# A joint attention and MLP stage: MLP halves for the last tile pair inside the loop, downs and outputs in groups of two or three matmuls, contexts laid out by tile

## The chip, the cores and the metric

The kernel runs on one core of one Trainium2 chip. The metric is the device time of one execution in microseconds (us), and the median over several executions is what is compared. One execution was profiled: its trace gives every instruction of the five engines (PE = TensorE matmuls, PEld = TensorE weight loads, DVE = VectorE, ACT = ScalarE, POOL = GpSimd) and of the DMA queues (SP issues nearly all of them).

## The reference

A decoder of two layers on x (16 x 128 tokens of 256 numbers, so 2048 rows, held as 16 tiles of 128). Each layer is attention, cross attention and an MLP, each followed by a sum with x and a layernorm. The changed stage is layer 0's cross attention together with layer 0's MLP:

```
q = _fq_sym((x @ Wq + bq) * scale);  k, v = _fq_sym of (ctx @ Wkv + bkv)      # 16 heads of 16
attn = softmax(q k^T)                       # every row attends to all 2048 context rows
attn = _fq_unsigned(attn)                   # steps of (row maximum)/255
x = layernorm(x + (attn v) @ Wp + bp)
gate, up = split(x @ w_gate_up.T);  x = layernorm(x + (silu(gate) * up) @ w_down.T)
```

## The kernel before

The phases follow one another: layer 0's attention (0 to 808 us), the keys and values of the cross attention (814 to 889 us), the **joint stage** (889 to 1712 us), then layer 1's attention, cross attention and mixture of experts. A phase takes its SBUF from a pool that is given back at its end, so the first loads of a phase wait for the last readers of the phase before.

**The loop of the joint stage.** `steps` has 128 entries: 8 pairs of tiles (`gp`), 8 pairs of heads (`i`), 2 tiles (`u`). A pair of tiles thus takes 16 steps, and a step has two halves (`part`, the two halves of the 2048 keys). Half e of step r of a pair is written (r, e) below, as `turn = (r, end)` in the code. In each half-step, in this order of the program:

- `scores` (L750): PE makes the scores of two heads for 1024 keys, in two tiles `s`. There are three `s` tiles of two PSUM banks.
- `scaled` (L757), twice: DVE scales a tile `s` into `e` and keeps the row maximum. Between the two calls DVE does whatever has been put off to this half-step (`due(at, "DVE")`).
- in the second half, the MLP's second matmul group (`ffn_half(..., 1, ...)`), where there is one;
- `context` (L800): PE's weighted sums for an earlier head pair, 0, 6, 5 and 5 matmuls in four half-steps in turn;
- `weights8` (L778): ACT's exponential to 8 bits for the step before, and a DMA that transposes it; `spread` (L790): POOL's cast of the transposed weights to bf16 for the step before that;
- `exponent` (L769), in the second half: ACT waits for DVE's maximum of the step;
- `pair_work` (L985): what the tile pairs before and after need, at fixed half-steps.

All five engines' instruction orders are written out by hand there (`manual_schedule`, L1053): an engine runs its instructions in the program's order, so PE cannot make the scores of half-step at+1 before the `pair_work` of half-step `at` is through. `later(at, engine, f)` puts a function off to a later half-step's place on that engine.

**What `pair_work` does** in a middle pair gp: the queries of the two tiles of pair gp+1 at (0,0) and (3,1) (`query`: PE L570, then DVE L577, L579, L587 and POOL L583 to L593); for pair gp-1 the reciprocal sums are transposed (`divided`, L821) at (4,1) and (5,0), the contexts are divided by DVE one half-step later (L826), multiplied with Wp (`put_out`, L832) at (5,1) and (6,0), added to x with the layernorm's statistics (`add_output`, L838, L136, L137), normalised by POOL (`norm_pair`, L142 to L149) and transposed (`transposed`, L155) at (7,1); its MLP's gate and up halves (`ffn_half`, L870) fill the steps 8 to 15; for pair gp-2 the MLP's down projection (`ffn_put_out`, L904, added at L912) is at (1,0), (2,0), (3,0) and (4,0), and its transposition at (6,1). All of these take their PSUM tile from the tag `misc`, which has **one buffer of one bank**: the next user of it waits until DVE or ACT has read the last one's result.

**The tail.** After step 127, nine more rounds of the loop without scores run the rest of the attention of pair 7 and, in `tail_work` (L1025), all 8 units of pair 6's MLP and its downs; pair 7's MLP stands after the loop, with the gate and up weights in one load of 2 MB (`ffn_load_all`, L856). The bias bp of the cross attention is loaded at the start and added to x by POOL (L548) after each of the four layernorms of the phase before.

## Time and profile before

| | us |
|---|---|
| median of 3 runs (lowest, highest) | 2769.02 (2765.05, 2771.07) |
| the profiled execution | 2766.96 |
| its span, first to last instruction | 2765.2 |
| PE / DVE / ACT / POOL busy | 2520.2 / 1910.0 / 1473.4 / 1205.5 |
| mean granted TensorE clock | 0.973 of full speed |
| first and last `scaled` of the joint stage begin | 890.3, 1638.9 |

The shares of busy time are means over phases with different limits; PE's 91% says nothing of the joint stage by itself. In rows of groups the columns are: line, engine, operation, output <- inputs, shapes, count, busy time, mean ns, then the idle time of the engine just before and what ended it.

### The profile page before, as it was taken

The numbers are of one execution on the slowest core, as the hardware profiler recorded it, in microseconds if no ns is written. First come the engines' busy times: TensorE is split into PE (matmuls) and PEld (weight loads), VectorE is DVE, ScalarE is ACT, GpSimd is POOL, SyncE is SP. The second block draws the span as 40 slices with busy tenths as digits, with TensorE's granted clock in tenths as the row PEclk, the third lists the DMA queues.
The fourth block names the chain that finished last, engine by engine and source line by source line (L and its number), as shares of the span: only waits on it lengthen the run. The fifth ranks groups of instructions, "written<-read, shape, count | busy, mean of one in ns | idle before, by whom it ended". The sixth has DMA issues, their size and how long they took to land.

```text
span 2765.2 us, 40096 instructions
## 1 busy us (share of the span) xinstructions
PE 2520.2 (91%) x14133; PEld 1510.0 (55%) x14164; DVE 1910.0 (69%) x4393; ACT 1473.4 (53%) x2778; POOL 1205.5 (44%) x1320
## 2 busy tenths in 40 slices
PE   5999999999976779988988878999988899999998
PEld 3677777777754234434443435566655546565746
DVE  5677777877747999899988972777777753323231
ACT  3455555555533888877977872555555432213120
POOL 5644545445426778878887862322232200000000
PEclk9999999999998799999999998999999999999999
DMA  7000000000010556565655552200010011111120
GB/s 225 1 1 1 1 1 1 1 1 1 1 51 25 107 113 113 119 113 103 132 117 104 112 109 77 110 1 2 2 54 11 4 57 51 50 43 57 36 65 12
DMA packets 360185, 150.86 MB, mean 55 GB/s; under 512 B 294576, under 2 KB 341136, under 8 KB 359472
## 3 DMA queue, kind: packets, MB, share of 16 engines
q1 hardware_dynamic: 358592, 144.49, 22.8%
q0 software_dynamic: 1392, 3.81, 0.6%
q8 instruction: 112, 1.84, 0.3%
q14 instruction: 89, 0.73, 0.1%
HBM read 74.71 MB, written 2.23 MB: 28 GB/s over the span
## 4 chain that ended last, share of the span: by engine, by line
PE 68%; DVE 11%; issue 7%; POOL 5%; ACT 5%; DMA 3%; SPq 0%; DVEq 0%; POOLq 0%; ACTq 0%
PE proj L339 11%; PE gate L1540 6%; PE py L1571 6%; PE up L1540 6%; DVE e L757 5%; PE po L466 4%; PE sc L1245 3%; PE tp L1265 3%; PE o L1275 3%; PE s L750 3%; PE sc L385 2%; POOL aT L790 2%; PE o L800 2%; PE pm L456 2%; PE pm L455 2%
## 5 line engine op out<-in xcount | busy, mean ns | idle before, releaser
L790 POOL CAST aT<-at 128x2048 bf16<-128x2048 uint8 x256 | 481.2, 1893 | 87.0 <-DMA at<-a 76.3
L778 ACT ACTIVATE a<-e,snl 128x2048 uint8<-128x2048 f32 x256 | 510.7, 1995 | 3.4
L757 DVE TENSOR_SCALAR_CACHE_REDUCE e<-s,qs,smx 128x1024 f32<-128x1024 f32 x256 | 336.4, 1338 | 30.1 <-PE s L750 29.8
L757 DVE TENSOR_SCALAR_CACHE_REDUCE e<-s,qs 128x1024 f32<-128x1024 f32 x256 | 319.5, 1279 | 36.1 <-PE s L750 31.6
L800 PE MATMUL o<-aT,vq 128*32 128x512 bf16 x1024 | 261.3, 390 | 1.8 <-POOL aT L790 1.8
L750 PE MATMUL s<-kT,qT 64*128 64x512 bf16 x1024 | 197.9, 398 | 41.7 <-DVE e L757 39.3
L1544 DVE TENSOR_TENSOR h<-h,up 128x512 f32<-128x512 f32 (+1 forms) x100 | 68.7, 687 | 192.7 <-PE up L1540 189.0
L1543 ACT ACTIVATE h<-gate 128x512 f32<-128x512 f32 (+1 forms) x100 | 59.7, 597 | 220.1 <-PE gate L1540 219.9
L800 PEld LDWEIGHTS <-vq 128*32 128x32 bf16 x1024 | 85.0, 97 | 162.3 <-issue 85.1
L1540 PE MATMUL gate<-xT,w_L_ffn_w1g 128*128 128x512 f32 x352 | 167.8, 595 | 0.0
L1540 PE MATMUL up<-xT,w_L_ffn_w1u 128*128 128x512 f32 x352 | 165.4, 592 | 0.0
L1254 DVE TENSOR_REDUCE amx<-sc 128x8 f32<-128x1024 f32 x96 | 116.7, 1216 | 64.7 <-PE sc L1245 64.6
L1571 PE MATMUL py<-w_L_ffn_w2T,h 128*128 128x256 f32 x704 | 154.6, 379 | 0.0
L1257 ACT ACTIVATE pr<-pr 128x1024 f32<-128x1024 f32 x96 | 101.6, 1059 | 88.4 <-DVE pr L1256 88.4
L1266 ACT COPY prT<-tp 128x512 f32<-128x512 f32 x192 | 104.3, 584 | 76.5 <-PE tp L1265 76.1
L1571 PEld LDWEIGHTS py<-w_L_ffn_w2T,h 128*128 128x128 f32 x704 | 133.7, 190 | 18.3
L870 PE MATMUL gu<-xT,wgu 128*128 128x256 f32 x440 | 126.2, 413 | 17.9 <-ACT xT L160 8.9
L750 PEld LDWEIGHTS <-qT 64*128 64x128 bf16 x1024 | 38.4, 94 | 163.7 <-issue 159.8
L409 ACT ACTIVATE pls<-sc,lm,rms_rs 128x128 f32<-128x128 f32 x256 | 113.8, 454 | 21.7 <-DVE lm L405 21.7
L339 PE MATMUL proj<-Wlk,xT 128*128 128x512 f32 x256 | 121.1, 595 | 3.5 <-DMA Wlk<-in_L_attn_Wlk 1.3
L339 PE MATMUL proj<-Wq,xT 128*128 128x512 f32 x256 | 122.1, 600 | 0.9 <-DVE raw_Wlk L348 0.9
L466 PE MATMUL po<-Wo,mT 128*128 128x256 f32 x512 | 121.2, 380 | 1.4 <-ACT mT L458 1.4
(313 smaller groups left out, 5477.6 us busy)
## 6 DMA issues: line engine op xcount, KB each, us to landing
wgu<-in_L_ffn_gu SPq DMA_DIRECT2D x112, 128.0 KB
sh<-share SPq DMA_DIRECT2D x32, 256.0 KB
at<-a SPq DMA_TRANSPOSE x256
sh<-share SPq DMA_DIRECT2D x16, 224.0 KB
sh<-share SPq DMA_DIRECT2D x16, 192.0 KB
w_L_ffn_w1g<-in_L_ffn_w1g SPq DMA_DIRECT2D x1, 2816.0 KB
w_L_ffn_w1u<-in_L_ffn_w1u SPq DMA_DIRECT2D x1, 2816.0 KB
w_L_ffn_w2T<-in_L_ffn_w2T SPq DMA_DIRECT2D x1, 2816.0 KB
```

What stands on the lines that cost most here:

```text
L339: nc.tensor.matmul(pp.rearrange("p h d -> p (h d)"), lhsT=xTt(b, k), rhs=wts[nm, hg][:, k, :], start=k == 0, stop=k == 1)
L409: nc.scalar.activation(pls[:, h, :], by_head[:, h // 2, h % 2, NC4:NK], AF.Exp, bias=nm[:, h : h + 1], scale=rq[:, h : h + 1], accum_out=s ...
L466: nc.tensor.matmul(outs[b], lhsT=st["mT"][:, h, :], rhs=wts["Wo", hg][:, h, :], start=hg == 0 and h == 0, stop=hg == 3 and h == 3,)
L750: nc.tensor.matmul(s[hh][:, c, :], lhsT=qT[t % 4][r, i, :], rhs=kT[r, i, at : at + G], start=True, stop=True)
L757: nc.vector.tensor_scalar(st["e"][hh][:, half, :], s[hh].rearrange("p a b -> p (a b)"), qs[2 * gp + u][:, 2 * i + hh : 2 * i + hh + 1], No ...
L778: nc.scalar.activation(a.bitcast(U8), st["e"][hh].rearrange("p a b -> p (a b)"), AF.Exp, bias=st["nm"][:, hh : hh + 1], accum_out=groups[g ...
L790: nc.gpsimd.tensor_copy(aT[:, :, hh, u * P : (u + 1) * P].rearrange("p (b j) q -> p b j q", j=2), st["at"][hh].bitcast(U8).rearrange("p b ...
L800: nc.tensor.matmul(o[r : r + 32].rearrange("p a b -> p (a b)"), lhsT=vq[:, n, 32 * i : 32 * i + 32], rhs=aT[:, n].rearrange("p a b -> p (a ...
L870: nc.tensor.matmul(ffn_ps[q][:, n, :], lhsT=wt[:, k, :], rhs=xT[q // 2][:, k, at], start=k == 0, stop=k == 1)
L1254: nc.vector.tensor_reduce(mx, sc, AX.X, ALU.max)
L1540: nc.tensor.matmul(pp[:rows], lhsT=wt[:, k, :], rhs=xT[g][:, k, :], start=k == 0, stop=k == 1)
L1571: nc.tensor.matmul(py, lhsT=h[:rows, i4 * P : (i4 + 1) * P], rhs=wt, start=n == 0, stop=n == len(parts) - 1)
```

## The change

- **MLP halves.** Pair 6's gate and up halves move from the tail into steps 8 to 15 of pair 7, as for the other pairs. The tail's units (`tail_unit`) go. The first three loads of a pair's gate and up weights are issued one half-step earlier.
- **Downs.** The 32 matmuls of 128x128 per tile pair, 8 at a time at four half-steps, become 16 of 128x256 at six half-steps, (1,0) to (3,1): 3, 3, 2, 3, 3, 2. Both tiles' results lie in one PSUM tile, with one add per tile (at (2,1) and (4,0)) in the place of two. `transposed` for pair gp-2 moves from (6,1) to (5,0).
- **Outputs.** 8 matmuls with Wp, 4 at (5,1) and 4 at (6,0), become 3, 3, 2 at (5,1), (6,0), (6,1), in one PSUM tile; the adds go to (6,1) and (7,0), `norm_pair` from (6,1) to (7,0).
- **Contexts by tile.** `ot` is laid out with the tile first; both tiles are divided by one DVE instruction of 128x1024 instead of two of 128x512, and their sums are transposed together at (4,1).
- **Query.** The second query moves from (3,1) to (4,0).
- **Tail.** Pair 6's downs are at (1,0), (1,1), (4,0) of the tail, pair 7's sums start two half-steps after the last step, its division is at (4,1), its outputs at (5,1) and (6,0); the last downs use 128x256 as well.
- **bp** is loaded in the joint stage's own pool and added by POOL at the beginning of the steps 0 to 15.

In the order of the instructions of the changed program PE waits for DVE before the ninth of the 16 downs (the first that writes the second tile's half) and before the seventh of the 8 outputs, and the first load of the keys' phase no longer stands behind additions of bp, of which there are none in the phase before any more; it waits for PE, among others.

```diff
@@ -204,7 +204,6 @@
         bo = load_row(pool, w["L0_attn_bo"], "bo0")
-        bp = load_row(pool, w["L0_xattn_bp"], "bp")
...
@@ -541,11 +540,7 @@
                 if n - 5 >= 0 and (n - 5) % 16 == 15:
-                    g = (n - 5) // 16
-                    layernorm(g, ps, "tp")
-
-                    for t in range(4 * g, 4 * g + 4):
-                        nc.gpsimd.tensor_tensor(xs[t], xs[t], bp, ALU.add)
+                    layernorm((n - 5) // 16, ps, "tp")
...
@@ -607,6 +602,7 @@
             wq = load_w(pool, "L0_xattn_Wq")
+            bp = load_row(pool, w["L0_xattn_bp"], "bp")
...
@@ -736,7 +732,7 @@
             ssum = stat.tile([P, 2, 16], F32, tag="ssum", name="ssum", bufs=3)
-            ot = wk.tile([P, 2, 2, 2 * P], F32, tag="ot", name="ot")
+            ot = wk.tile([P, 2, 2, 2, P], F32, tag="ot", name="ot", bufs=1)
...
@@ -811,28 +807,30 @@
         def sums_by_dim(gp, u):
-            rb = wk.tile([P, 16, 16], F32, tag="rb", name="rb", bufs=1)
+            rb = wk.tile([P, 16, 16], F32, tag="rb", name="rb")
...
-        def sums_T(rb):
-            pt = ps.tile([P, 2, P], F32, tag="misc", name="pt_r")
-            for c in range(2):
-                nc.tensor.transpose(pt[:, c, :], rb[:, 8 * c : 8 * c + 8, :].rearrange("p h d -> p (h d)"), ident)
+        def sums_T(rbs):
+            pt = ps.tile([P, 2, 2, P], F32, tag="misc", name="pt_r")
+            for u, rb in enumerate(rbs):
+                for c in range(2):
+                    nc.tensor.transpose(
+                        pt[:, u, c, :], rb[:, 8 * c : 8 * c + 8, :].rearrange("p h d -> p (h d)"), ident
+                    )
...
-        def divide(gp, u, pt):
-            own = groups[gp][2][:, :, :, u * P : (u + 1) * P]
-            nc.vector.tensor_tensor(own, own, bc(pt, 2, 2), ALU.mult)
-
-        def output(gp, u):
+        def divide(gp, pt):
+            ot = groups[gp][2].rearrange("p u c h q -> p (u c) h q")
+            nc.vector.tensor_tensor(ot, ot, bc(pt.rearrange("p u c q -> p (u c) q"), 2, 2), ALU.mult)
+
+        def output(gp, js, py):
             ot = groups[gp][2]
-            py = ps.tile([P, HID], F32, tag="misc", name="py")
-            for c in range(4):
+            for j in js:
+                u, c = j // 4, j % 4
                 nc.tensor.matmul(
-                    py, lhsT=ot[:, c // 2, c % 2, u * P : (u + 1) * P], rhs=wp4[:, c, :], start=c == 0, stop=c == 3
-                )
-            return py
+                    py[:, u, :], lhsT=ot[:, u, c // 2, c % 2, :], rhs=wp4[:, c, :], start=c == 0, stop=c == 3
+                )
...
@@ -895,23 +893,19 @@
-        def ffn_down(q, u, c, tag="misc"):
-
-            at = slice(c * P, (c + 1) * P)
-            pp = ps.tile([P, 2, G] if tag == "s" else [P, P], F32, tag=tag, name="pd", bufs=3 if tag == "s" else 1)
-            pd = pp[:, 0, 0:P] if tag == "s" else pp
-            for i in range(NI):
+        def ffn_down_psum(tag="misc"):
+            pp = ps.tile([P, 2, G] if tag == "s" else [P, G], F32, tag=tag, name="pd", bufs=3 if tag == "s" else 1)
+            return (pp[:, 0] if tag == "s" else pp).rearrange("p (u d) -> p u d", u=2)
+
+        def ffn_down(q, js, pd):
+            for j in js:
+                u, i = j // NI, j % NI
                 nc.tensor.matmul(
-                    pd, lhsT=hs[q][:, i, u * P : (u + 1) * P], rhs=wd[:, i, at], start=i == 0, stop=i == NI - 1
-                )
-            return pd
-
-        def ffn_add(q, u, c, pd):
-            t = 2 * q + u
-            x = xs[t][:, c * P : (c + 1) * P]
-            nc.vector.tensor_tensor(x, x, pd, ALU.add)
-            if c == 1:
-                norm_pair_stats(t)
+                    pd[:, u], lhsT=hs[q][:, i, u * P : (u + 1) * P], rhs=wd[:, i, :], start=i == 0, stop=i == NI - 1
+                )
+
+        def ffn_add(q, u, pd):
+            add_output(2 * q + u, pd[:, u])
...
@@ -948,29 +942,45 @@
-        def divided(gp, u, at):
-
-            pt = sums_T(rbs.pop((gp, u)))
-            later(at + 1, "DVE", divide, gp, u, pt)
-
-        def put_out(gp, u, at):
-            py = output(gp, u)
-            later(at + 1, "DVE", add_output, 2 * gp + u, py)
-            if u == 1:
+        def divided(gp, at):
+
+            pt = sums_T([rbs.pop((gp, u)) for u in range(2)])
+            later(at + 1, "DVE", divide, gp, pt)
+
+        pys = {}
+
+        def put_out(gp, js, at):
+
+            if 0 in js:
+                pys[gp] = ps.tile([P, 2, HID], F32, tag="misc", name="py")
+            output(gp, js, pys[gp])
+            for u in range(2):
+                if 4 * u + 3 in js:
+                    later(at + 1, "DVE", add_output, 2 * gp + u, pys[gp][:, u])
+            if 7 in js:
...
             ffn_gate(q, i, n)
+            if 2 * i + n + 3 < 2 * NI:
+                ffn_load(2 * i + n + 3)
...
-        def ffn_put_out(q, u, c, at, tag="misc"):
-            pd = ffn_down(q, u, c, tag)
-            later(at + 1, "DVE", ffn_add, q, u, c, pd)
-            if (u, c) == (1, 1):
+        pds = {}
+
+        def ffn_put_out(q, js, at, tag="misc"):
+
+            if 0 in js:
+                pds[q] = ffn_down_psum(tag)
+            ffn_down(q, js, pds[q])
+            for u in range(2):
+                if NI * u + NI - 1 in js:
+                    later(at + 1, "DVE", ffn_add, q, u, pds[q])
+            if 2 * NI - 1 in js:
...
@@ -987,61 +997,42 @@
             turn = (r, end)
-            if gp < LAST and turn in ((0, 0), (3, 1)):
-                query(2 * gp + 2 + r // 3, at)
+            if gp < LAST and turn in ((0, 0), (4, 0)):
+                query(2 * gp + 2 + r // 4, at)
             if gp > 0:
-                if turn in ((4, 1), (5, 0)):
-                    divided(gp - 1, r - 4, at)
-                elif turn in ((5, 1), (6, 0)):
-                    put_out(gp - 1, r - 5, at)
+                if turn == (4, 1):
+                    divided(gp - 1, at)
+                elif turn in ((5, 1), (6, 0), (6, 1)):
+                    j = 3 * (2 * r + end - 11)
+                    put_out(gp - 1, range(j, min(j + 3, 8)), at)
...
                     transposed(gp - 1, at)
-            if 0 < gp < LAST:
-                j = 2 * (r - 8) + end
-                if -3 <= j < 0:
-                    ffn_load(j + 3)
+                if turn in ((6, 0), (6, 1), (7, 0)):
+                    ffn_load(2 * r + end - 12)
...
                     ffn_half(gp - 1, r - 8, 0, at)
-                    if j + 3 < 2 * NI:
-                        ffn_load(j + 3)
-
-            if 1 < gp <= LAST:
-                if not end and 1 <= r <= 4:
-                    ffn_put_out(gp - 2, (r - 1) // 2, (r - 1) % 2, at)
-                elif turn == (6, 1):
+
+            if gp > 1:
+                if (1, 0) <= turn <= (3, 1):
+                    j = (0, 3, 6, 8, 11, 14, 16)[2 * r + end - 2 :]
+                    ffn_put_out(gp - 2, range(j[0], j[1]), at)
+                elif turn == (5, 0):
...
-
-        def tail_unit(q, i, at, stream):
-            for m in range(2):
-                ffn_gate(q, i, m, "s")
-                if stream and 2 * i + m + 3 < 2 * NI:
-                    ffn_load(2 * i + m + 3)
-            th, gu = ffn_tiles(q, i, tail=True)
-            ffn_out(q, th, gu)
-            ffn_sigmoid(th)
-            later(at + 1, "DVE", ffn_mult, q, i, th, gu, nc.vector)
...
             turn = (r, end)
-            q = LAST - 1
-            if turn in ((1, 0), (1, 1), (2, 0)):
-                for i in range(2):
-                    tail_unit(q, 2 * (2 * r + end - 2) + i, at, True)
-            elif turn == (3, 1):
-                tail_unit(q, 6, at, True)
-            elif turn in ((4, 0), (4, 1)):
-                divided(LAST, end, at)
-                if end:
-                    tail_unit(q, 7, at, True)
-            elif turn in ((5, 0), (5, 1)):
-                put_out(LAST, end, at)
-            elif r == 6:
-                for c in range(2):
-                    ffn_put_out(q, int(end), c, at, "s")
+            if turn in ((1, 0), (1, 1), (4, 0)):
+                j = {(1, 0): (0, 4), (1, 1): (4, 8), (4, 0): (8, 16)}[turn]
+                ffn_put_out(LAST - 1, range(*j), at, "s")
+            elif turn == (4, 1):
+                divided(LAST, at)
+            elif turn in ((5, 1), (6, 0)):
+                j = 4 * (r - 5)
+                put_out(LAST, range(j, j + 4), at)
...
@@ -1056,6 +1047,8 @@
                         group(n // 16)
+                    if n < NB:
+                        nc.gpsimd.tensor_tensor(xs[n], xs[n], bp, ALU.add)
...
@@ -1071,10 +1064,8 @@
                     gp, r = n // 16, n % 16
-                    if part == 1 and 0 < gp < LAST and r >= 8:
+                    if part == 1 and 0 < gp <= LAST and r >= 8:
                         ffn_half(gp - 1, r - 8, 1, at)
-                        if 2 * (r - 8) + 4 < 2 * NI:
-                            ffn_load(2 * (r - 8) + 4)
...
@@ -1088,11 +1079,17 @@
                                 if i % 4 == 3:
-                                    later(at + 1, "ACT first", nc.scalar.copy, groups[gp][2][:, i // 4], os.pop((gp, i // 4)))
-                                if i == 7:
+                                    later(
+                                        at + 1,
+                                        "ACT first",
+                                        nc.scalar.copy,
+                                        groups[gp][2][:, :, i // 4].rearrange("p u h q -> p h u q"),
+                                        os.pop((gp, i // 4)).rearrange("p h (u q) -> p h u q", u=2),
+                                    )
+                                if i == 7 and gp < LAST:
...
                                     for u in range(2):
-                                        later(at + 1 + u, "POOL", by_dim, gp, u)
+                                        later(at + 1, "POOL", by_dim, gp, u)
...
@@ -1108,14 +1105,14 @@
                     due(at, "SP")
+                    if (n, part) == (len(steps), 1):
+                        later(at + 1, "DVE", sums, LAST)
+                        for u in range(2):
+                            later(at + 2, "POOL", by_dim, LAST, u)
...
                         tail_work(n, bool(part))
-                    if n == len(steps) - 2 + part:
-                        ffn_load(part)
-                if n == len(steps) - 1:
-                    ffn_load(2)
...
@@ -1130,9 +1127,9 @@
             for u in range(2):
-                for c in range(2):
-                    ffn_add(LAST, u, c, ffn_down(LAST, u, c, "s"))
-            norm_pair(LAST)
+                ffn_put_out(LAST, range(NI * u, NI * u + NI), 0, "s")
+                due(1, "DVE")
+            due(1, "POOL")
```

## The prediction

> **What bounds the kernel now.** I read the page's groups first, then busy time by stretches of the joint stage, then DVE's timeline and waits in one tile pair, then the chain of waits at both ends of the stage. The groups give the two costliest DVE rows:
>
> ```profile
> L757 DVE TENSOR_SCALAR_CACHE_REDUCE e<-s,qs,smx 128x1024 f32<-128x1024 f32 x256 | 336.4, 1338 | 30.1 <-PE s L750 29.8
> L757 DVE TENSOR_SCALAR_CACHE_REDUCE e<-s,qs 128x1024 f32<-128x1024 f32 x256 | 319.5, 1279 | 36.1 <-PE s L750 31.6 <-ACT snl L769 2.2 <-ACT gu_s L889 1.6
> ```
>
> DVE is the loop's pacemaker, and 61.4 us of its idle time end with scores from PE. Where, by stretches: steps 0-7 and 8-15 of pair 4, steps 8-15 of pair 7, and the tail (from, to and length, then busy PE, PEld, DVE, ACT and POOL, the granted clock, DMA):
>
> ```profile
> 1262.01:1314.21 52.20, 43.34 (x228) 20.92 (x228) 46.89 (x88) 36.26 (x44) 41.40 (x42) 0.97 0.48 92
> 1314.21:1358.19 43.98, 41.55 (x192) 18.02 (x192) 40.65 (x66) 43.03 (x65) 38.44 (x30) 1.00 0.74 144
> ...
> 1600.60:1640.30 39.70, 29.89 (x125) 8.26 (x125) 39.64 (x66) 35.78 (x43) 30.52 (x17) 0.96 0.58 112
> 1640.30:1711.80 71.50, 60.01 (x312) 46.58 (x310) 22.61 (x55) 25.51 (x56) 13.31 (x20) 0.93 0.24 68
> ```
>
> With nothing beside it DVE needs 39.7 for eight steps (third line). The first eight of a pair lose time on both accounts: more DVE work and DVE idle. DVE's timeline shows the two largest holes of pair 4 (start, length, idle before), and its waits in 1262 to 1314.2 the sum of all five:
>
> ```profile
> 1300.20 1.28 DVE L757 TENSOR_SCALAR_CACHE_REDUCE e<-s,qs 128x1024 f32<-128x1024 f32 x1 [1.52 <-PE s L750]
> ...
> 1305.75 1.34 DVE L757 TENSOR_SCALAR_CACHE_REDUCE e<-s,qs,smx 128x1024 f32<-128x1024 f32 x1 [2.03 <-PE s L750]
> ```
> ```profile
> DVE e L757 <- PE s L750: 5.2, 5, 2.0
> ```
>
> The two follow the outputs at (5,1) and (6,0), a third of 1.09 at 1288.96 the downs at (4,0): in each PE stands in front of the one `misc` bank until DVE has emptied it, then makes its matmuls, and only then the next scores. The same wait in the first eight steps of pairs 2 to 6 is 7.2, 6.0, 5.2, 5.6 and 6.1 (30.1), of pair 1 2.2, of pair 7 2.9: 35.2 in all.
>
> The chain at the stage's beginning, and in its tail:
>
> ```profile
> 805.49 2.01 PE po L466 x8
> ...
> 811.86 2.09 POOL x L548 x3
> 813.97 0.38 SPq L89
> ...
> 814.40 7.43 DMA ctxT<-in_ctxT
> ```
> ```profile
> 1665.67 8.44 DMA wgu_all<-in_L_ffn_gu
> ...
> 1681.56 7.14 PE pd L904 x64
> ...
> 1689.81 14.10 PE gu L870 x64
> ```
>
> The keys' phase begins when the last addition of bp gives the pool free. The tail is a chain of loads, contexts (PE o L800, 3.56 for 16) and MLP matmuls, with the transfer of 2 MB open in it.
>
> **The change, part by part** (us; minus is a gain).
>
> *MLP halves into pair 7: +4.8.* Eight such steps take 43.98 (pair 4) or 44.94 (pair 5), without halves 39.70; the mean difference is 4.8, the bounds 4.3 and 5.3. SP's 16 loads more stand among the transposes as in pairs 1 to 6, so that price holds them. The loads' earlier start puts one issue of 0.57 (SP at 1305.21) ahead of a transpose: nothing, since the cast that uses it runs a half-step ahead of the contexts.
>
> *The loop's first eight steps: -22.6.* Of the seven users of `misc` that remain in a pair (query, downs, query, sums, transposition, outputs, transposition; twelve before), I follow PE and DVE through the half-steps. PE needs 0.45 for the scores (four matmuls, two at a time), 0.216 for a context, 0.43 for a matmul with Wp or a down of 128x256 (two records of 0.216 each); DVE 2.41 and 2.53 for a half-step, 0.84 more for a query, 1.01 for an add with statistics (1301.41 to 1302.43). (1,0): 0.45 + 5 x 0.216 + 3 x 0.43 = 2.8 of PE against 2.41 of DVE, but PE comes out of (0,1), where DVE takes 3.3 and PE 1.75, with its scores done, and (2,0) costs PE 1.3: no idle to (2,1). There the ninth down waits for the add of the first tile, which ends 1.65 after the half-step's start; with three downs and the scores PE then comes 0.5 late in (3,0). (4,0) and (4,1): add and query on DVE cover PE's wait for each. (5,0): the division ends 2.45 after the start, transposition 0.45, scores 0.45 and their latency 0.39 against DVE's 3.7: 0.2 late at most. (6,1): the last two outputs wait for the first tile's add too, but DVE's own 3.5 there covers PE's 3.1. (7,1): statistics end 2.3 after (7,0) begins, POOL's `norm_pair` takes 2.6 (1292.03 to 1294.66), the transposition then ends 2.0 after (7,1) begins: 0.4 late. That is 1.1 per pair. POOL's cast behind this `norm_pair` comes 1.9 late, and its contexts are 5 us away; price if that cover went, the same 1.9 per pair. `ot`'s single buffer is read last at (6,1) and written again at (12,0): nothing.
>
> To the 1.1 I add 0.9 for TensorE's clock. After a stretch with long holes PE runs at half speed for one stretch of 3.4:
>
> ```profile
> 1299.40:1302.84 3.44, 1.63 (x9) 0.98 (x9) 2.57 (x6) 3.44 (x3) 3.35 (x4) 1.00 0.14 27
> 1302.84:1306.26 3.42, 3.42 (x11) 1.40 (x10) 1.39 (x3) 0.29 (x2) 1.18 (x1) 0.50 0.96 194
> ```
>
> New holes of 2.1 stand at (5,0) (PE behind the division) and (7,1), so I keep about one such stretch per pair; it costs at most half of itself, 1.7, and 0.9 is the middle between that and none. New idle 2.0 in each of pairs 2 to 7 and 1.2 in pair 1, 13.2 against 35.2: -22.0. DVE's own work: adds 0.20 + 0.88 + 0.20 + 0.88 become 2 x 1.01, and the divisions 0.54 + 0.60 one of 128x1024, by the nearest row (L1256) 1.22 less the 0.1 that overlaps: -0.1 per pair, -0.6. Bounds: 0, if the new waits are as long as the old, and -35.8, if none is left.
>
> Two rules of the Trainium skill bear on this. The Trainium skill's page "TensorE: Matmul & The Clock Gate" (Why this matters for your kernels) asks for no PE-idle gap over some 3 us between bursts. The row above speaks against reading that as enough: PE's longest gap before the half-speed stretch was 1.8 (1300.07 to 1301.88). By the rule the 0.9 goes and the sum is 6 lower; by the row it stays. The Trainium skill's page "PSUM — Partial Sum Buffer" (PSUM bank collisions raise a hardware error) says that accesses of two engines must be kept apart by bank and quadrant, not by address. That speaks against two tiles' downs in one bank: it is the wait of the ninth down. No run here shows that wait; separate banks would save the 0.5 per pair, 3 in all.
>
> *bp: -6.3.* With no addition left, the first load waits for PE's last matmul at 807.5 in place of POOL at 813.97, and everything to the loop follows 7.4 of ctxT: -6.4, less the 0.1 of the semaphore. If it waits for ACT's xT (812.1), -1.9; I take the first, since PE stands among that load's waits and the layernorm's tiles lie in no pool that is given back. The 16 additions (0.722 each, 11.6) go to POOL's steps of pair 0, where POOL has two casts, 3.8 of 4.94: nothing; uncovered it would be 11.6.
>
> *The tail: -18.4.* Before: 71.6 from DVE's last score (1640.16) to 1711.80. After: the last cast ends 9.7 after that score (1649.87); contexts 3.6; eight downs of pair 6, 3.5; sums' transposition 0.45, then add and division on DVE 2.2; outputs 3.6; add and statistics 1.05; `norm_pair` 2.65; transposition and copy 1.2; gates 14.1; downs 6.9; add 0.5: 49.4. The 2 MB are issued when the previous cast tile is read (some 7 after the score) and land 8.4 later, 11 before the gates. PE stands idle for 3.4, 2 and 5 us on the way, so half speed comes back: +4, between 0 and 8 (contexts doubled 3.6, gates 3.4, outputs 1). 71.6 - 53.4 = 18.2, with 0.2 for the adds halved.
>
> *Query at (4,0):* the same instructions, its DMA one half-step later and nine steps before its reader: nothing.
>
> Sum: 4.8 - 22.6 - 6.3 - 18.4 = -42.5. From the profiled execution (2766.96) that is 2724.5; the median of the runs stands 2.1 above that execution: **2726**.
>
> **Rivals.**
> 1. *Half speed eats the loop's gain.* Two more half-speed stretches per pair at the full 1.7, 3.4 x 5 = 17: 2743. For it: PE is emptier than before at (4,0) and (7,0). Against: of the fifteen stretches of 3.4 in pair 4's first eight steps one was slow.
> 2. *PE stays at full speed*: idle 0.5 per pair, the tail without its 4: -32.3 - 22.4 - 6.4 + 4.8 = -56: 2713. For it: the downs fill (1,0) to (3,1) more evenly. Against: the half-speed row above. With gaps of 2.1 the loop would also stay warm by the Trainium skill's page "TensorE: Matmul & The Clock Gate" (Why this matters for your kernels).
> 3. *Slower: the one `misc` bank.* If each of the five hand-overs from (2,1) to (7,1) costs what the worst cost before (2.03), DVE idles 10 in each of 7 pairs, 70 against 35.2: +35 + 4.8 - 6.3 - 18.4 = +15: 2784. It decides from (35.2 + 19.9) / 7 = 7.9 per pair, 1.6 per hand-over. For it: downs and outputs now hold the bank for six and three half-steps. Against: nobody else asks for it there.
>
> **How the numbers follow.** Chances: forecast 0.62 (own range 2714 to 2738), rival 1 0.17, rival 2 0.13, rival 3 0.06, no change 0.02. 2708 to 2748 takes in the forecast and most of rivals 1 and 2 with the bounds of the tail. A difference of 0.2% (5.5 us) is about what a measurement here tells from none. Faster 0.92, within 0.02, slower 0.06.
>
> **What will show it.** DVE's wait for scores in a pair's first eight steps near 2 in place of 6; pair 7's second eight near 44.5; the first load of the keys at 807.6; from the last score to the stage's end near 53. I am wrong if the holes at (5,0) and (7,1) exceed 1, if half-speed stretches come twice a pair, or if the loop's POOL falls behind its casts.

## The result

The changed kernel takes 2731.06 us (median of 4 runs, 2727.62 to 2733.81) against 2768.49 for the kernel before in the same comparison (4 runs, 2765.05 to 2771.07): a ratio of **0.9865, with the 95% interval 0.9848 to 0.9882**, some 37 us faster. The forecast was 2726, with the range 2708 to 2748. Its profiled execution took 2732.66, with a span of 2730.9. Below, "loop" is the time from the first `scaled` row's start to the last one's end, "tail" from there to the end of the stage's last down; all times are in us.

| profiled executions | before | changed | moved | forecast |
|---|---|---|---|---|
| first `scaled` row begins | 890.3 | 882.6 | -7.7 | -6.3 |
| loop, pair 0 | 84.2 | 81.6 | -2.7 | 0 |
| loop, first eight steps of pairs 1 to 7 | 360.4 | 344.7 | -15.7 | -22.6 |
| loop, second eight steps of pairs 1 to 7 | 305.3 | 312.5 | +7.2 | +4.8 |
| tail | 71.5 | 56.3 | -15.2 | -18.4 |
| all behind it | 1053.5 | 1053.2 | -0.3 | 0 |
| sum | | | -34.3 | -42.5 |

Every term that was forecast has the sign and the order of size of the forecast; three of them are 2 to 7 worse. The parts are read from one execution of each kernel: the first `scaled` row begins at 882.6 to 885.3 in the thirteen kernels below that have the new loading of bp, so a unit or two of a part can be chance.

The two costliest DVE rows of the changed kernel, from the page's groups:

```profile
L753 DVE TENSOR_SCALAR_CACHE_REDUCE e<-s,qs,smx 128x1024 f32<-128x1024 f32 x256 | 335.0, 1334 | 16.9 <-PE s L746 15.9
...
L753 DVE TENSOR_SCALAR_CACHE_REDUCE e<-s,qs 128x1024 f32<-128x1024 f32 x256 | 319.8, 1280 | 36.7 <-PE s L746 31.2
```

DVE's wait for scores has fallen from 61.4 to 47.1. The stretches that answer to those of before are the first and the second eight steps of pair 4, the second eight of pair 7, and the tail (from, to and length, then busy PE, PEld, DVE, ACT and POOL, the granted clock, DMA):

```profile
1242.14:1292.47 50.33, 43.23 (x196) 18.76 (x196) 47.13 (x84) 36.43 (x46) 41.23 (x42) 0.97 0.55 105
1292.47:1338.36 45.89, 44.37 (x192) 19.16 (x192) 40.65 (x64) 42.94 (x65) 39.14 (x30) 0.93 0.64 127
1575.75:1621.40 45.65, 44.07 (x190) 19.17 (x191) 40.64 (x64) 42.69 (x64) 39.13 (x30) 0.93 0.62 128
1621.40:1677.70 56.30, 45.30 (x184) 32.30 (x182) 13.43 (x35) 17.02 (x35) 15.30 (x22) 0.91 0.22 52
```

In the first line DVE idles 3.2 (50.33 less 47.13) where it idled 5.3. In the second and third the granted clock is 0.93, where it was 1.00 and 0.96: the second eight steps of pairs 1 to 7 now hold nine stretches of 3.4 at half speed where they held four, and that is part of their 7.2. DVE's timeline of pair 4 shows what became of the two holes of 1.52 and 2.03; these are now the three longest of its first eight steps, and the waits of the same stretch sum them up:

```profile
1262.65 1.34 DVE L753 TENSOR_SCALAR_CACHE_REDUCE e<-s,qs,smx 128x1024 f32<-128x1024 f32 x1 [0.62 <-PE s L746]
...
1273.12 1.28 DVE L753 TENSOR_SCALAR_CACHE_REDUCE e<-s,qs 128x1024 f32<-128x1024 f32 x1 [0.57 <-PE s L746]
...
1280.21 1.28 DVE L753 TENSOR_SCALAR_CACHE_REDUCE e<-s,qs 128x1024 f32<-128x1024 f32 x1 [0.62 <-PE s L746]
```
```profile
DVE e L753 <- PE s L746: 2.3, 5, 0.6
DVE e L753 <- ACT snl L765: 0.4, 1, 0.4
```

Holes of 1.5 to 2 have become holes of 0.6, and one of 0.4 in which DVE waits for ACT's `exponent` of the step before.

On PE the change is less plain. These are PE's waits in the first eight steps of pair 5 (1338.36 to 1389.12): in us, how many, and the longest.

```profile
PE pq L565 <- DVE x L836: 1.8, 1, 1.8
PE ln_pt L155 <- POOL x L149: 1.6, 2, 1.4
PE ln_pt L155 <- DVE ot L825: 1.5, 1, 1.5
PE pd L903 <- DVE x L836: 0.8, 1, 0.8
PE py L831 <- DVE x L836: 0.8, 1, 0.8
PE pq L565 <- ACT gu_s L887: 0.5, 1, 0.5
```

They sum to 7.0; the same stretch of the kernel before has 8.6 in nine rows. So PE still stands in front of the one `misc` bank: at (4,0) for the query behind the downs' last add, at (5,0) for the division, and at (2,1) and (6,1) for the first tile's add. At (7,1) it waits not for the bank but for `norm_pair` on POOL. What was won is that DVE notices it less.

At the boundary, SP's queue and its waits show the first load of the keys, 7.0 earlier than at 813.97:

```profile
806.93 0.38 SPq L89 DMA_DIRECT2D w_L_xattn_Wkv<-in_L_xattn_Wkv  x1
```
```profile
SPq L89 <- PE po L465: 5.1, 1, 5.1
```

It waits for PE's last matmul of the phase before, as forecast.

### The profile page after: what moved, and what is told of

The parts are those of the page before. It is cut to its first block, busy times and chain, and to the rows that moved or that the text cites. A ratio compares the mean times of both kernels' runs of the same rounds, so it can differ in the third digit from the quotient of the medians.

```text
span 2730.9 us, 39531 instructions
## 1 busy us (share of the span) xinstructions
PE 2518.5 (92%) x13877; PEld 1493.5 (55%) x13908; DVE 1902.3 (70%) x4353; ACT 1473.7 (54%) x2778; POOL 1215.0 (44%) x1336
## 5 line engine op out<-in xcount | busy, mean ns | idle before, releaser
L746 PE MATMUL s<-kT,qT 64*128 64x512 bf16 x1024 | 191.0, 397 | 31.8 <-DVE e L753 28.7
L868 PE MATMUL gu<-xT,wgu 128*128 128x256 f32 x448 | 135.4, 427 | 9.2 <-ACT xT L160 4.3
L1253 DVE TENSOR_TENSOR pr<-sc,amx 128x1024 f32<-128x1024 f32 x96 | 117.0, 1219 | 5.7
```

The lines of the kernel that those rows point to most:

```text
L746: nc.tensor.matmul(s[hh][:, c, :], lhsT=qT[t % 4][r, i, :], rhs=kT[r, i, at : at + G], start=True, stop=True)
L868: nc.tensor.matmul(ffn_ps[q][:, n, :], lhsT=wt[:, k, :], rhs=xT[q // 2][:, k, at], start=k == 0, stop=k == 1)
L1253: nc.vector.tensor_tensor(pr, sc, bc(mx, 2, P), ALU.subtract)
```

## The experiments

Each kernel ran beside the kernel before on the same chip, in four comparisons in which the kernel before took 2765.5 to 2770.2; so times of different rows are best compared by their ratios. Medians, ratios to the kernel before with their 95% intervals, and loop and tail of the profiled execution:

| kernel | median | ratio | loop | tail |
|---|---|---|---|---|
| before | 2768.5 | 1 | 750.0 | 71.5 |
| changed | 2731.1 | 0.9865 [0.9848, 0.9882] | 738.8 | 56.3 |
| bp alone, on the kernel before | 2761.4 | 0.9968 [0.9957, 0.9979] | 752.5 | 71.7 |
| changed, MLP of pair 6 in the tail | 2741.3 | 0.9897 [0.9875, 0.9919] | 730.9 | 70.6 |
| changed, downs with a pause | 2733.2 | 0.9883 [0.9866, 0.9899] | 737.6 | 59.8 |
| changed, transposition moved | 2731.0 | 0.9880 [0.9866, 0.9895] | 743.1 | 56.8 |
| changed, outputs in two half-steps | 2728.1 | 0.9865 [0.9851, 0.9880] | 731.5 | 56.9 |
| changed, PE's wait at (7,1) filled | 2726.0 | 0.9857 [0.9843, 0.9872] | 730.6 | 54.5 |
| the same, half the filling (one execution) | 2726.1 | | 732.9 | 55.0 |
| three waits filled | 2718.7 | 0.9817 [0.9801, 0.9832] | 726.8 | 54.0 |
| (7,1) filled, DVE's small work first | 2719.4 | 0.9819 [0.9801, 0.9837] | 725.4 | 53.0 |
| the same with half the downs | 2715.6 | 0.9805 [0.9782, 0.9828] | 719.9 | 54.9 |
| the same (all downs), and the tail reworked | 2718.2 | 0.9818 [0.9801, 0.9834] | 725.8 | 50.9 |
| changed, DVE's small work first | 2718.5 | 0.9817 [0.9800, 0.9833] | 723.8 | 57.0 |

Two of them undo or isolate whole parts of the change; the others ask why loop and tail gained less than was forecast. The theory after the first reading was the clock: PE's waits at (4,0) and (7,1) set off half speed behind them. Its rivals were the wait of the ninth down for the shared bank, and plain work: PE has as much to do in these steps as DVE.

### bp alone

The row bp is loaded beside Wq and added in pair 0 instead of after the layernorms of the phase before, and `ot` has one buffer (the load and `ot` are not shown):

```
                         group(n // 16)
+                    if n < NB:
+                        nc.gpsimd.tensor_tensor(xs[n], xs[n], bp, ALU.add)
...
-                    for t in range(4 * g, 4 * g + 4):
-                        nc.gpsimd.tensor_tensor(xs[t], xs[t], bp, ALU.add)
```

> The kernel before with the bp part alone: the row of bp loaded with the joint stage's weights, its sixteen additions in the steps of pair 0 on POOL, and ot in one buffer so that the row finds room. In the kernel before the first scaled row stands at 890.3 and pair 0 takes 84.2; in the changed kernel 882.6 and 81.6. Theory A, the boundary's gain is the early give-back of the pool and nothing else of the change bears on it: the first scaled row at 882.6, pair 0 between 81.6 and 84.2, all behind it as in the kernel before, the time 7 to 10 below it (ratio 0.9965 to 0.9975). Theory B, POOL pays for the additions in pair 0 (11.6 in all): pair 0 at 86 or more, and the ratio 0.998 to 1.002.

The first `scaled` row begins at 883.9, 6.4 earlier; pair 0 takes 83.2; the time falls by 8.8. Theory A holds, and POOL does not pay for the additions. The 0.3% is a gain of its own.

### The MLP of pair 6 back in the tail

```
-                if r >= 8 and not end:
+                if gp < LAST and r >= 8 and not end:
                     ffn_half(gp - 1, r - 8, 0, at)
...
-            if turn in ((1, 0), (1, 1), (4, 0)):
-                j = {(1, 0): (0, 4), (1, 1): (4, 8), (4, 0): (8, 16)}[turn]
-                ffn_put_out(LAST - 1, range(*j), at, "s")
+            if turn in ((1, 0), (1, 1), (2, 0)):
+                for i in range(2):
+                    tail_unit(q, 2 * (2 * r + end - 2) + i, at, True)
+            elif turn == (3, 1):
+                tail_unit(q, 6, at, True)
...
+                if r == 6:
+                    ffn_put_out(q, range(16), at, "s")
```

> The changed kernel with the MLP of the last pair but one put back where the kernel before has it: no halves in pair 7's second eight, its units in the tail between the contexts, its loads there; downs, outputs and the rest of the loop stay as changed. In the changed kernel pair 7's second eight take 45.7 and the tail (last scaled row to the last down) 56.3; in the kernel before 39.7 and 71.5. Theory A, the halves cost 4.3 to 6 in pair 7 and save 13 to 16 in the tail: second eight at 39.7 to 40.5, tail at 69 to 72, the time 8 to 11 above the changed kernel. Theory B, half of the 6 is the half speed that the wait at (7,1) leaves behind at (8,0), and comes without halves too: second eight at 42 to 43, the time 11 to 14 above. Theory C, the tail's gain comes mostly from its own new order: tail at 60 to 64, the time at most 3 above.

The second eight steps of pair 7 and the tail of this kernel:

```profile
1575.07:1615.99 40.92, 32.40 (x125) 8.45 (x124) 39.79 (x64) 35.55 (x42) 30.72 (x17) 0.83 0.53 103
1615.99:1686.63 70.64, 60.49 (x248) 44.60 (x247) 22.36 (x51) 25.54 (x56) 13.33 (x18) 0.93 0.25 70
```

40.9 against 45.7 with the halves, and 70.6 against 56.3: the halves cost 4.7 and save 14.3, and the time is 10.2 above the changed kernel's (8.9 by the ratios). Theory A holds with its second eight steps 0.4 over the bound; C falls. B asked for 42 to 43 and gets only its cause: there is half speed here too, but with no gates to make DVE hardly feels it (39.79 busy of 40.92).

### Downs with a pause

```
-                    j = (0, 3, 6, 8, 11, 14, 16)[2 * r + end - 2 :]
+                    j = (0, 4, 8, 8, 11, 14, 16)[2 * r + end - 2 :]
```

> The changed kernel with the downs at another pace: four each at (1,0) and (1,1), none at (2,0), then three, three and two at (2,1), (3,0) and (3,1), so that the first tile's add at (2,0) has the bank for itself. The loop (first scaled row to the end of the last) takes 738.7 in the changed kernel, and its half-steps (1,0) to (3,1) take 17.7 in the mean of pairs 2 to 6; DVE's own work in them is 15.8. Theory A, the ninth down's wait for the shared bank (0.85 of PE, and what follows it) is the loss: the six half-steps take 16.3 to 16.8, about 1.1 less in each of six pairs, and the loop 732. Theory B, PE has too much to do in these half-steps, whatever the order (four downs, five contexts and the scores are 3.25 of PE against 2.47 of DVE): the holes move to (1,1) and (2,0), the six half-steps stay within 0.3 of 17.7, the loop at 737 to 740.

The half-steps (1,0) to (3,1) of pair 5, here first in the changed kernel, then with the pause:

```profile
1344.09:1361.75 17.66, 16.61 (x77) 7.88 (x76) 16.42 (x32) 13.36 (x17) 15.02 (x13) 1.00 0.59 112
```
```profile
1341.70:1359.36 17.66, 16.25 (x77) 7.99 (x76) 16.38 (x32) 13.36 (x17) 14.32 (x12) 1.00 0.54 104
```

PE's wait of 0.8 at the ninth down is gone from its list, and the six half-steps take 17.66 as before. The hole has moved, as DVE's timeline shows: it now idles before (2,0), after four downs each at (1,0) and (1,1). PE's scores begin at 1343.41 and 1347.05 with no wait between them, so such a half-step is 3.64 of PE, and not the 3.25 of the expectation:

```profile
1347.79 1.28 DVE L753 TENSOR_SCALAR_CACHE_REDUCE e<-s,qs 128x1024 f32<-128x1024 f32 x1 [1.00 <-PE s L746]
```

Theory B holds. The wait of the ninth down was there and cost nothing that this other order of the downs gives back.

### The transposition moved out of (5,0)

```
-                elif turn == (5, 0):
-                    transposed(gp - 2, at)
+                elif gp > 2 and turn == (0, 1):
+                    transposed(gp - 3, at)
```

> The changed kernel with the transposition after the downs taken from (5,0), between the division's factors and the outputs, to (0,1) of the next pair (for the last pair into the tail). In the changed kernel PE waits 1.9 at (5,0) for the division to give the bank free, and (5,0) and (5,1) take 3.77 and 3.31 in the mean of pairs 2 to 6; DVE's work in them is 3.6 and 2.5. Theory A, a user of the bank fewer between division and outputs saves its wait: 0.8 to 0.9 less in each of six pairs at (5,0) and (5,1), little at (0,1), whose query makes DVE slow anyway, and the loop takes 734. Theory B, the wait only moves: (0,1) and (1,0), now 3.32 and 2.41, become 0.5 to 1 longer since the transposition waits for the query's read and the first down for the copy behind it, and the loop takes 737 to 741.

(5,0) and (5,1) take 0.93 less in the mean of pairs 2 to 6 (3.54 and 2.61), and (1,0) and (1,1) 0.88 more (2.94 and 3.22). PE's waits in the first eight steps of pair 5 say the same; the division's 1.5 is gone, and in its place the same transposition waits for the query's read:

```profile
PE ln_pt L155 <- DVE qa L572: 0.9, 1, 0.9
```

The wait only moved: theory B. The loop is 4.3 longer than the changed kernel's in these two executions: pair 0, which the edit does not touch, takes 3.0 more, (8,0) and (8,1) together 3.2 more (half speed stands there in six of seven pairs, in four of them for two stretches), and the first eight steps 2.4 less. The median is the same, the ratio 0.9880 against 0.9865 with intervals that overlap.

### Outputs in two half-steps

```
-                elif turn in ((5, 1), (6, 0), (6, 1)):
-                    j = 3 * (2 * r + end - 11)
-                    put_out(gp - 1, range(j, min(j + 3, 8)), at)
+                elif turn in ((5, 1), (6, 0)):
+                    j = 4 * (r - 5)
+                    put_out(gp - 1, range(j, j + 4), at, 2)
```

The last argument puts the first tile's add a half-step later, beside the second one's.

> The changed kernel with the outputs in two half-steps, four at (5,1) and four at (6,0), both adds at (6,1), and norm_pair behind them at (6,1) in place of (7,0). In the changed kernel (5,1) to (8,1) take 22.3 in the mean of pairs 2 to 6, of which DVE's work is some 19.3, and the loop 738.7. Theory A, norm_pair at (7,0) is too late for the transposition at (7,1), and PE's wait there sets off the half speed at (8,0) and (8,1): both go, (8,0) and (8,1) take 5.5 in place of 6.5, (7,1) 2.6 in place of 3.0, the seven half-steps 20.5, and the loop loses 9 to 12, to some 728. Theory B, PE's work is what counts and the half speed comes from how little PE has to do in (6,1) and (7,0) rather than from the wait: (8,0) and (8,1) stay at 6.5 or rise, four outputs in a half-step make holes of 1 to 2 at (5,1) and (6,0) as in the kernel before, and the loop takes 738 to 746.

(8,0) and (8,1) take 5.1 to 5.7 in six of seven pairs and 7.3 in one; before this edit 5.4 to 8.3. (5,1) to (8,1) take 21.7 in place of 22.3, with (6,1) at 4.50 for its two adds. The loop of the profiled execution falls by 7.3: theory A in kind, smaller in size, since the half speed has in part only moved to (7,0) (three pairs). The time does not show it: the ratio is that of the changed kernel.

### PE's wait at (7,1) filled

```
     def norm_pair_T(q, psum, tag, fill=0, w=None):
         pt = psum.tile([P, 2, 2, P], F32, tag=tag, name="ln_pt")
+        for _ in range(fill):
+            nc.tensor.matmul(pt[:, 0].rearrange("p a b -> p (a b)"), lhsT=ident, rhs=w[:, 0, :], start=True, stop=True)
```

with `fill` = 4 at (7,1) and the weights `wp4`; a second kernel has `fill` = 2.

> The changed kernel with four matmuls of 128x256 (1.7 of PE) more at (7,1), ahead of the transposition, into the tile that the transposition then writes over: they have no use but to keep PE busy while it waits for POOL's norm_pair; the output is the same. Theory A, the wait at (7,1) sets off the half speed behind it: the stretches of half speed at (7,1) to (8,1) (in six of seven pairs) go, (8,0) and (8,1) take 5.5 in every pair in place of 8.3 in pairs 1, 4 and 7 and 6 in the others, and the loop loses 8 to 12, from 738.7 to about 729. Theory B, (8,0) and (8,1) are long for the gates' own reasons (they wait for the copy of xT, and for the one bank between two units), whatever the clock: no change, 738 to 740, or up to 3 more where the fillers come late.

> The changed kernel with two filling matmuls (0.86) at (7,1) in place of four (1.7) or none; PE then stands idle there for some 0.6 in place of 1.4. Theory A, it is the length of the wait that sets off the half speed, and 0.6 is short enough (waits of 0.5 to 0.8 stand at (2,1) and (6,1) in every pair without a slow stretch behind them): (8,0) and (8,1) at 5.4 in every pair as with four. Theory B, it is PE's share of work in the stretch, and half of it is too little: one or two of the seven pairs still show 6 to 8.3.

PE's timeline of pair 4 around (7,1), in the changed kernel and with four filling matmuls (L154, two records each; contexts, scores and gates stand two lines lower there, at L798, L748 and L870):

```profile
1288.03 1.25 PE L796 MATMUL o<-aT,vq 128*32 128x512 bf16 x5
1290.70 0.33 PE L155 MATMUL ln_pt<-ident,x 128*128 128x128 f32 x1 [1.43 <-POOL x L149]
...
1293.07 2.07 PE L868 MATMUL gu<-xT,wgu 128*128 128x256 f32 x4 [0.74 <-ACT xT L160]
```
```profile
1285.69 1.25 PE L798 MATMUL o<-aT,vq 128*32 128x512 bf16 x5
1286.88 1.99 PE L154 MATMUL ln_pt<-wp,ident 128*128 128x256 f32 x8
1288.71 0.76 PE L157 MATMUL ln_pt<-ident,x 128*128 128x128 f32 x4
1289.40 0.61 PE L748 MATMUL s<-kT,qT 64*128 64x512 bf16 x4
1290.74 1.13 PE L870 MATMUL gu<-xT,wgu 128*128 128x256 f32 x4 [0.73 <-ACT xT L162]
```

The same four gate matmuls take 2.07 and 1.13. (8,0) and (8,1) together, with the clock in the column behind the engines:

```profile
1292.47:1300.76 8.29, 7.69 (x23) 3.33 (x24) 5.12 (x9) 7.04 (x10) 6.13 (x4) 0.59 0.55 105
```
```profile
1290.14:1295.54 5.40, 4.80 (x23) 2.19 (x24) 5.03 (x8) 5.40 (x9) 4.24 (x3) 1.00 0.45 83
```

With the filling, both half-steps take 5.38 to 5.41 in all seven pairs, where the changed kernel has 5.4 to 8.3; the loop falls by 8.2, to 730.6. Theory A was 729. Two filling matmuls do the same (5.39 to 5.43 in every pair; the loop's 732.9 has a pair 0 that took 3.2 longer with the same code). So work without any use makes these half-steps shorter, and the cause is the clock and not the gates' own waits: the wait of 0.73 for ACT's copy is still there. In the time the gain is not clear of noise: 0.9857 against 0.9865, some 2 us, with overlapping intervals; the runs with more filling show it.

### Three waits filled

To the four at (7,1) come four filling matmuls at (4,0) ahead of the query, into the score tile that is used next, and eight ahead of the tail's transposition.

> The kernel with the four filling matmuls at (7,1), four more at (4,0) of pairs 2 to 6 ahead of the query (into the score tile that comes next) and eight ahead of the transposition in the tail (PE stands idle there for 3.4). With the fillers at (7,1) alone the loop takes 730.6, with half speed after (4,0) in three pairs, and the tail 54.5. Theory A, each wait of PE of 1.8 to 3.4 sets off the half speed behind it, and any work in it prevents that: no half speed in (4,0) to (4,1) and none in the tail's gates, loop 727 to 729 and tail 52.5 to 53.5, 3 to 5 less in all. Theory B, only the wait at (7,1) mattered, since (4,0) has slack behind it: loop 730 to 732, tail at 54 to 55.

The loop takes 726.8, with one stretch of half speed left, at (5,0) of pair 7, and none in the tail's gates; the tail, 54.0, keeps half speed in its contexts. Theory A, with the tail 0.5 over its bound. In all, fillers took 11.9 from the loop (1.7 from the first eight steps of pairs 1 to 7, 10.0 from the second eight): that is what half speed costs the changed kernel there, less what the fillers themselves take. The time agrees: from 0.9865 to 0.9817, 13 us. Even so the first eight steps of pairs 2 to 5 take 49.5, with 47.0 of DVE's work: **2.5 of idle time per pair that the clock has no part in**.

### DVE's small work first

```
-                        scaled(*now, part, 0, states[n], s)
                         due(at, "DVE")
+                        scaled(*now, part, 0, states[n], s)
                         scaled(*now, part, 1, states[n], s)
```

This was run together with the fillers at (7,1), and by itself on the changed kernel.

> The kernel with the four filling matmuls at (7,1), and in addition DVE's small work of a half-step (adds, query, division) ahead of both scaled rows instead of between them. With the fillers alone the loop takes 730.6. Theory A, PE's waits for DVE's read of the one bank (0.85 at (2,1), 1.9 at (4,0), 1.9 at (5,0), 0.9 at (6,1)) are what is left of the loss, and DVE reading 1.3 earlier takes most of them: 2 to 3 less in each of six pairs, loop 713 to 719. Theory B, PE's work in these half-steps is the bound and the scores come late either way; DVE's small work first only holds back the release of the score tiles: the loop between 728 and 736.

> The changed kernel with DVE's small work of a half-step ahead of both scaled rows, without any filling matmul. With the fillers too the loop takes 725.4, with the fillers alone 730.6, the changed kernel 738.7. Theory A, the earlier read of the bank shortens PE's wait at (4,0) and (5,0), and with norm_pair 1.3 earlier that at (7,1), so that the half speed goes by itself: loop 725 to 729 and (8,0) and (8,1) at 5.1 to 5.4. Theory B, the wait at (7,1) stays near 1 to 1.4 and with it the half speed: (8,0) and (8,1) at 6 to 8 in most pairs, loop 732 to 737.

By itself it beats the changed kernel and the one with the fillers at (7,1): 2718.46, and the loop takes 723.8. The first eight steps of pairs 1 to 7 fall from 344.7 to 332.9, DVE's idle time in them from 19.5 to 10.0. PE's waits in pair 5 (1335.57 to 1383.76) are of another kind now:

```profile
PE s L746 <- DVE e L753: 3.6, 6, 1.4
PE ln_pt L155 <- DVE ot L825: 0.7, 1, 0.7
PE pq L565 <- DVE x L836: 0.5, 1, 0.5
```

The waits of the kinds shown for the changed kernel have fallen from 7.0 to 1.2; for the rest PE waits until DVE has emptied a score tile, so it runs ahead and DVE sets the pace. From pair 1 on no stretch of the loop is at half speed any more. But the clock is the smaller part in the first eight steps: the fillers took 1.7 from them, this order 11.8, so most of that is the order itself. That is theory A; only (8,0) and (8,1) are at 5.7 where 5.1 to 5.4 was expected. Together with the fillers the kernel has no half speed either, but 725.4, between its two theories: with the small work first `norm_pair` comes earlier, the four fillers end too late for the transposition, and (7,1) takes 3.74 in place of 2.60. Three waits filled and small work first end at the same ratio, 0.9817, and the second adds no work.

### Half the downs

```
                 u, i = j // NI, j % NI
+                if i % 2 and q < LAST - 1:
+                    continue
```

> The kernel with the four filling matmuls at (7,1) and DVE's small work first, with every second down of the pairs 0 to 5 left out (eight of sixteen matmuls; their share of the MLP's sum is missing from the output). That is 3.45 less of PE in (1,0) to (3,1) of pairs 2 to 7, with the same hand-overs, the same adds and the same work on DVE. Theory A, in these half-steps PE's work at full speed is the bound, not the waits: the twelve rows from the one of (1,0) to the last of (3,1), now 18.4, shrink by 1.5 to 2.6 to about 16.2 (DVE's own work is 15.8), and the loop from 725.4 to 710 to 716. Theory B, the hand-overs of the bank are the bound: at most 0.5 less per pair, loop 722 to 725.

The rows from (1,0) to (3,1) with all downs (pair 5), and with half of them (pair 4), both at full speed:

```profile
1338.68:1357.11 18.43, 17.86 (x84) 8.68 (x82) 17.25 (x34) 14.25 (x18) 15.09 (x13) 1.00 0.55 107
```
```profile
1243.79:1261.21 17.42, 15.23 (x67) 6.01 (x66) 17.09 (x35) 14.25 (x18) 14.11 (x12) 1.00 0.55 107
```

1.0 less, and 0.8 in the mean of pairs 2 to 7: between the two theories. The expectation had DVE's own work wrong: it is 17.1 in these rows (with the small work first the query's read and the second add fall into them), not 15.8. Measured by DVE's idle time, 1.18 becomes 0.33 with the same hand-overs of the bank: most of what idle time there is comes from PE's work and not from the bank, in this order of DVE's. In pairs 2, 4, 5 and 7 half speed came back, where PE was emptier and nothing else was changed, and took part of the gain; the loop won 5.4.

### The tail reworked

Small work first and four fillers at (7,1); in the tail six fillers into the free bank ahead of the last contexts, eight ahead of the transposition, and the two tiles' outputs in two banks.

> The kernel with the four filling matmuls at (7,1) and DVE's small work first, and in addition three things in the tail: six filling matmuls into the free misc bank while PE waits for the last casts, eight ahead of the last transposition, and the outputs of the two tiles in two score tiles in place of one bank, so that the second tile's do not wait for the first one's add. Without these the loop takes 725.4 and the tail 53.0. Theory A, the tail is a chain on PE with half speed after two of its waits and one hand-over of the bank (0.5 of wait and more behind it): tail 49 to 51, the time 2 to 4 below the 2719.4 of the kernel without them, 2715 to 2717. Theory B, the fillers end too late for what they wait beside, or the clock has recovered before the gates: tail 52.5 to 54, the time at 2718 to 2721.

PE's timeline of the tail in the changed kernel, from the last contexts on, and of this one:

```profile
1632.83 5.30 PE L796 MATMUL o<-aT,vq 128*32 128x512 bf16 x16 [2.97 <-POOL aT L786]
...
1644.16 1.99 PE L831 MATMUL py<-wp,ot 128*128 128x256 f32 x8 [1.94 <-DVE ot L825]
1646.67 1.99 PE L831 MATMUL py<-wp,ot 128*128 128x256 f32 x8 [0.51 <-DVE x L836]
1652.02 1.44 PE L155 MATMUL ln_pt<-ident,x 128*128 128x128 f32 x4 [3.36 <-POOL x L149]
```
```profile
1617.36 2.75 PE L1039 MATMUL warm<-wp,ident 128*128 128x256 f32 x12
1620.28 3.61 PE L798 MATMUL o<-aT,vq 128*32 128x512 bf16 x16 [0.17 <-POOL aT L788]
...
1629.92 3.72 PE L833 MATMUL py<-wp,ot 128*128 128x256 f32 x16 [1.94 <-DVE ot L827]
```

The contexts take 3.61 in place of 5.30, the outputs have no wait between the tiles, and the tail takes 50.9 in place of 53.0 without the three edits: theory A in the trace. In the time it does not show: 2718.15 against 2719.44 with intervals of 4 to 5 on either side.

## Why the prediction was right, and where its steps were off

**The sign, the range and the bound.** DVE was the pacemaker, its holes came from PE standing in front of the one bank, and the change took most of them. The time lies 5 above the forecast.

**MLP halves into pair 7 (+4.8): right.** The experiment that takes them out again gives 4.7. The trace has 6.0, and two stretches of half speed in pair 7's (8,0) and (8,1); with the wait at (7,1) filled the same eight steps take 42.8 to 43.1, which is 3.1 to 3.5 above the kernel before. So half speed is 2.5 to 2.9 of the 6.0, less what the fillers take.

**bp (-6.3): right.** -7.7 in the trace, -6.4 in the kernel that changes nothing else, -5.0 to -7.7 in all thirteen kernels that have it. The choice between PE (807.5) and ACT (812.1) as the last reader was right: the first load stands at 806.93.

**The loop's first eight steps (-22.6): the mechanism right, the term too large by 6.9.** Measured -15.7: DVE's idle time fell by 16.5 (36.0 to 19.5) and its work rose by 0.8. Three parts of the step were off.

- "No idle to (2,1)", and 0.5 at (3,0). In (1,0) to (3,1) DVE idles 1.24 (17.66 less 16.42). The price of PE was too low: a half-step with five contexts and three downs was put at 2.8, and it takes 3.24 at full speed and without a wait (the rows of (1,1) of pair 5 stand below this list; its scores begin at 1345.38, the next ones at 1348.62). DVE needs 2.41 there, so PE falls behind by 0.8 and not by 0.4, and its lead is gone sooner. Over the six half-steps PE is busy for 16.25 to 16.61 and DVE for 16.4: two engines with equal work that wait for each other now and then cannot both be full. The pause shows that moving the one named wait gives nothing, and the run with half the downs (with DVE's small work first) shows in DVE's idle time that it is mostly PE's work.
- New idle 1.1 per pair without the clock. With the waits filled it is 2.5, what the fillers themselves hold up included; this is the largest error of the sum. In pair 4 the holes stand before (3,1), (5,0) and (6,0), 0.62, 0.57 and 0.62 long, and before (8,0), 0.25. The second one stands behind the waits at (4,0) and (4,1), which were to be covered by DVE's add and query. All are below 1, the bound that was set for (5,0) and (7,1).
- The clock, 0.9 per pair in the first eight steps. There it was too much: only three stretches of half speed stand in these steps (six in the kernel before), and filling takes 1.7 from them where the sum has 5.4 (six times 0.9). But the loop has twelve in the seven pairs, 1.7 per pair, and nine of them stand behind the wait at (7,1), in (8,0) and (8,1). There they lengthen the second eight steps, which the sum has as unchanged in pairs 1 to 6. That the two errors on the clock and on PE's price go opposite ways in the first eight steps is luck. Rival 1 named the clock, and half-speed stretches "twice a pair" was one of the signs against the forecast: 1.7 comes close to it. Yet the kernel before has ten of them in the same pairs, so the change added two and moved the others.

PE's timeline of (1,1) of pair 5 in the changed kernel, for the first of the three:

```profile
1345.38 0.64 PE L746 MATMUL s<-kT,qT 64*128 64x512 bf16 x4
1345.95 1.25 PE L796 MATMUL o<-aT,vq 128*32 128x512 bf16 x5
1347.13 1.56 PE L903 MATMUL pd<-w_L_ffn_d,h 128*128 128x256 f32 x6
1348.62 0.61 PE L746 MATMUL s<-kT,qT 64*128 64x512 bf16 x4
```

**The tail (-18.4): too large by 3.2.** Contexts begin 11.4 behind the last score and not 9.7, because POOL does the last unit's two `ffn_mult` rows (0.73 each) ahead of the last casts: work that the change itself had moved there. The outputs take 4.5 in place of 3.6, with the second tile waiting 0.51 for the first one's add in the shared bank; transposition and copy take 2.1 in place of 1.2, gates 15.8 in place of 14.1. The allowance of 4 for half speed held the gates' 1.7 and the contexts' 1.7.

**Pair 0 (nothing forecast, -2.7).** Not a gain of the change: with the same work in pair 0, the kernels run here take 81.1 to 85.0 there. It goes with how long pair 0 is at half speed: the kernels at 81.1 to 81.6 have 24 to 27 us of it at half speed, those at 84.2 to 85.0 37 to 41.

**The two rules.** What the Trainium skill's page "PSUM — Partial Sum Buffer" (PSUM bank collisions raise a hardware error) asks for shows here as a wait that the program makes, and not as a loss: the ninth down's 0.8 is in the trace, and a kernel without it is no faster. The Trainium skill's page "TensorE: Matmul & The Clock Gate" (Why this matters for your kernels) asks for no PE-idle gap over some 3 us; here the measurement decides against it as sufficient: the stretch from 1288.99 to 1292.40, whose longest gap was 1.43, was followed by 6.8 us of half speed, and filling that gap removed it in every pair. What I held against rival 1 (one slow stretch in fifteen before) counted stretches and did not ask how full they were.

**What stays open.** How the 2.5 of idle time divides between PE's work, the hand-overs of the bank and ACT's `exponent` (0.4 per pair in the waits) was only argued: half the downs point at PE's work, the small work first at the hand-overs. And why one order gives a stretch just under half full that is followed by half speed and another, equally full, one that is not.

## What to carry to other kernels

When two engines have nearly equal work and one shared bank between them, do the short read that frees the bank first and the long rows after it: one line moved took 13 us off the changed kernel (by the ratios), where another pace of the downs took nothing. Ask of every wait of TensorE not how long it is but how full it leaves the 3.4 us around it, since what comes behind a stretch that is only half full can run at half speed; that loss shows up in the next stage, not where the wait stands. And price a matmul by the distance between two starts in the trace, with what stands around it. And when work is moved into a loop's last steps, look at what it puts ahead of the tail's first instruction on each engine.

## What the hardware showed that was not expected

**The clock goes by fixed stretches of 3.41 us and by how busy PE was in the one before.** In the changed kernel, half speed in the loop always begins a whole number of 3.413 us after an earlier one (1080.77, 1104.67, 1268.51, 1292.40, 1364.08, 1387.97) and lasts one or two of them. Busy times by these stretches around pair 4's (7,1), PE in the first column and the clock behind POOL's:

```profile
1285.57:1288.99 3.42, 3.42 (x18) 0.99 (x14) 3.35 (x8) 2.70 (x4) 1.94 (x3) 1.00 0.90 187
1288.99:1292.40 3.41, 1.71 (x10) 0.57 (x8) 3.23 (x6) 1.82 (x3) 3.22 (x6) 1.00 0.66 138
1292.40:1295.82 3.42, 2.75 (x8) 1.31 (x8) 2.50 (x4) 3.42 (x5) 3.42 (x3) 0.50 0.28 54
1295.82:1299.23 3.41, 3.41 (x9) 1.60 (x8) 2.62 (x4) 2.19 (x5) 1.86 (x2) 0.50 0.54 117
1299.23:1302.64 3.41, 3.41 (x17) 1.39 (x15) 1.89 (x3) 3.38 (x5) 1.31 (x2) 1.00 0.75 116
```

Here half a stretch of work is followed by a slow one, and a slow stretch that is not full by another. In the fourteen profiled kernels a slow stretch was followed by another in 13 of 86 cases, in all of them with PE busy for 0.69 to 0.86 of the first; none of the fuller ones was. With the four fillers the stretch over the same wait holds 3.33 of PE and the next one runs at full speed. Over the loops of all fourteen, from pair 1 on, a full-speed stretch was followed by a slow one in 20 of 20 cases where PE was busy for less than 0.45 of it, in 26 of 35 from 0.45 to 0.5, in 26 of 117 from 0.5 to 0.6, in 1 of 100 from 0.6 to 0.7, and in none of 2299 above. The longest gap does not tell them apart: it was 0.7 to 2.2 in the stretches that were followed by half speed, and up to 1.8 in those that were not. The Trainium skill's page "TensorE: Matmul & The Clock Gate" (What's actually happening) describes such a free-running window of 3413 ns; the traces agree with the window, and add that half of one idle can be enough.

A consequence: the same wait costs or does not cost by where it falls. In the changed kernel PE's wait for the query at (4,0) is 1.8 in pairs 2 to 5 and 2.2 in pair 6, and half speed followed it in pairs 2, 4 and 5 but not in pairs 3 and 6.
